# Seven block products for the spreads of layers 1 to 3, and layer 0's candidate kept in PSUM

## The chip, the cores and the metric

The kernel runs on one core of a Trainium2 chip. The metric is device time in microseconds (us), from the start of a launch to its end; a profiled span is about 1.8 us shorter than the time of the same run.

## The reference, cut to what matters

64 samples of 256 nodes by 128 features pass through four graph layers in float32. Each layer ends in a residual layer norm. All samples share one 256x256 adjacency matrix.

```python
# layer 0, five steps (in_matrix = out_matrix = adj)
m  = einsum('nm,bmd->bnd', adj, h)               # "spread"
z  = sigmoid(av @ w3.T + u3(h)); r = sigmoid(av @ w4.T + u3(h))
hv = tanh(av @ w5.T + (r * h) @ u5.T)            # "candidate"
h  = (1 - z) * h + z * hv
# layer 1: one spread over the off-diagonal weights    (q1 in the kernel)
# layer 2: attention, then one spread over A_final     (g)
# layer 3: adj, adj^2 and adj^3 applied to x, weighted (q3 is the first)
x = layernorm(x + layer(x))                      # after every layer
```

## The kernel before: what the change and the argument touch

The samples are taken in 32 pairs. The kernel first lists all its operations, each with one or more ways (engine, expected microseconds, function). A planner inside the kernel then puts them into one fixed order, with one fixed tile for each value. Two of its tables:

```python
CLASSES = {"X": (512, 15), ..., "A": (512, 30), ..., "PS": (512, 8), ...}   # tiles: size, how many
USES = {"DVE+": ("DVE", "PORT"), "POOL": ("POOL", "PORT"), "POOL-": ("POOL",)}
```

`X` holds the 15 pairs in flight, `A` the shared SBUF tiles, `PS` eight tiles of PSUM, the banks (SBUF and PSUM are the memories in which the kernel has its tiles; all 7196 pass records of the kernel before write PSUM). A way marked `DVE+` is a VectorE operation on two SBUF operands, but for some normalizations and relus on one. The planner books it on VectorE and on a PORT, which GpSimd's sums use too: it never plans the two for the same time.

A spread comes in two forms. The plain one is two batches by two block rows, each against 256 columns. The other, in the manner of Strassen and Winograd, takes seven block products of 128 columns, with sums of blocks before, between and after them:

```python
def spread(i, right):                    # 4 products of 256 columns
    t = bank()
    for b in range(2):
        def fn(b=b):
            for j in range(2):
                nc.tensor.matmul(t.at(2, N)[:, b, :], tokens(i)[:, 2*b+j, :], right.ap[:, j, :], ...)
        pe(mm(512), fn, [i, right, *[t] * b], [t])
    return t

def spread7(h, right, terms):            # 7 products of 128 columns
    sv, o, t = Value("A", name="sums"), Value("A", name="mT"), bank()
    def sum_(us, us_pool, fn, r, w):
        S.add([("DVE+", us, ...), ("POOL", us_pool, ...)], r, w)
    sum_(...)  sum_(...)  sum_(...)                        # sums of h
    product(0) product(1) product(3) product(2)            # into the four quarters of one bank
    evacuate(o <- t)                                       # copy, ScalarE or VectorE
    sum_(sv <- o, o)
    product(0) product(3) product(1)                       # on top of the same bank
    sum_(o3 <- sv, sv);  evacuate(o0 <- t0);  dve(o1, o2 <- t1, t3, sv)
    return o
```

A spread of this form is called a seven below. Before the change only layer 0 used `spread7`, in 150 places; the other 106 spreads were plain. The end of a step of layer 0 was:

```python
act(tanh: hv <- t)                       # bank t is free from here on
dve2(hv <- hv - hT)                      # dve2 = "DVE+": SBUF, SBUF
dve2(hv <- (z + 1) * hv)
dve2(hT <- 0.5 * hv + hT)
```

## Time and profile before

| | before |
|---|---|
| time | 1494.5 us (1494.3 to 1494.62, 3 runs) |
| TensorE busy | 1485.7 of 1493.0 us, 7196 pass records |
| VectorE, ScalarE, GpSimd busy | 1227.4, 974.7, 701.5 us |
| passes of 128, 256, 512 columns, start to start | 0.1117, 0.216, 0.43 us |

A float32 product leaves two pass records: the 106 plain spreads, 424 products, left 848. The end of a matmul record is modelled and reaches past the start of the next (records of 128, 256 and 512 columns last 275, 379 and 592 ns, each 0.163 us more than their spacing), so a busy share near 100% can hide short pauses. The sound way is to take the distance from start to start for each width and to add these up. What is left over are pauses.

### The profile page before, as it was taken

The numbers are of one execution on the slowest core, as the hardware profiler recorded it, in microseconds if no ns is written. First come the engines' busy times: TensorE is split into PE (matmuls) and PEld (weight loads), VectorE is DVE, ScalarE is ACT, GpSimd is POOL, SyncE is SP. The second block draws the span as 40 slices with busy tenths as digits, with TensorE's granted clock in tenths as the row PEclk, the third lists the DMA queues.
The fourth block names the chain that finished last, engine by engine and source line by source line (L and its number), as shares of the span: only waits on it lengthen the run. The fifth ranks groups of instructions, "written<-read, shape, count | busy, mean of one in ns | idle before, by whom it ended". The sixth has DMA issues, their size and how long they took to land.

```text
span 1493.0 us, 26228 instructions
## 1 busy us (share of the span) xinstructions
PE 1485.7 (100%) x7196; PEld 1058.8 (71%) x7196; DVE 1227.4 (82%) x3041; ACT 974.7 (65%) x2860; POOL 701.5 (47%) x964
## 2 busy tenths in 40 slices
PE   9999999999999999999999999999999999999998
PEld 6555666666677777767667677776677767788997
DVE  7776988999989888887888888788788887889752
ACT  3444555666677776766666767577576667777874
POOL 3432543565566544445354444444345534356442
PEclk9999999999999999999999999999999999999999
DMA  8553556778789887777668876867678766677862
GB/s 233 109 107 74 118 120 128 142 145 160 157 162 177 163 179 152 151 162 160 135 135 170 154 143 132 169 150 164 138 142 163 157 136 135 130 147 164 160 125 64
DMA packets 949475, 217.02 MB, mean 145 GB/s; under 512 B 728144, under 2 KB 944848, under 8 KB 949328
## 3 DMA queue, kind: packets, MB, share of 16 engines
q1 hardware_dynamic: 949328, 215.34, 71.2%
q8 instruction: 58, 0.95, 0.3%
q14 instruction: 89, 0.73, 0.2%
HBM read 117.12 MB, written 98.11 MB: 144 GB/s over the span
## 4 chain that ended last, share of the span: by engine, by line
PE 100%; POOLq 0%; ACT 0%; DVE 0%; issue 0%; ACTq 0%; POOL 0%
PE ps L563 16%; PE ps L545 12%; PE ps L689 9%; PE ps L696 9%; PE ps L681 9%; PE ps L697 9%; PE ps L682 9%; PE ps L718 8%; PE ps L788 4%; PE ps L832 4%; PE ps L824 4%; PE ps L825 4%; PE ps L748 2%; PE ps L520 0%; PE ps L295 0%; PE ps L456 0%
## 5 line engine op out<-in xcount | busy, mean ns | idle before, releaser
L235 ACT COPY a<-ps 128x512 f32<-128x512 f32 (+2 forms) x465 | 210.8, 461 | 166.7 <-PE ps L545 48.3
L563 PEld LDWEIGHTS ps<-aTt,a 128*128 128x128 f32 x1140 | 167.8, 192 | 45.2 <-issue 38.0
L685 ACT ACTIVATE a<-ps,bzrh 128x512 f32<-128x512 f32 x160 | 109.8, 686 | 121.9 <-PE ps L682 105.2
L563 PE MATMUL ps<-aTt,a 128*128 128x128 f32 x1140 | 188.9, 275 | 0.0
L699 ACT ACTIVATE a<-ps,bzrh 128x512 f32<-128x512 f32 x160 | 109.9, 687 | 112.2 <-PE ps L697 107.2
L696 PE MATMUL ps<-a,w 128*128 128x512 f32 x320 | 163.6, 593 | 0.0
L697 PE MATMUL ps<-a,u5h 128*128 128x512 f32 x320 | 163.4, 592 | 0.0
L682 PE MATMUL ps<-a,w 128*128 128x512 f32 x320 | 163.4, 592 | 0.0
L689 PE MATMUL ps<-a,w 128*128 128x512 f32 x320 | 162.4, 593 | 0.0
L582 POOL TENSOR_TENSOR a<-a 128x128 f32<-128x128 f32 x132 | 80.9, 614 | 168.1 <-DVE a L578 154.4
L642 ACT ACTIVATE a<-ps 128x128 f32<-128x128 f32 x460 | 121.1, 282 | 54.9 <-PE ps L788 26.0
L563 PEld LDWEIGHTS ps<-aT,a 128*128 128x128 f32 x780 | 125.1, 191 | 42.2 <-issue 36.6
L526 DVE STREAM_TRANSPOSE a<-a 128x512 f32<-128x512 f32 x217 | 150.7, 698 | 4.8 <-PE ps L689 1.0
L718 PEld LDWEIGHTS ps<-W,a 128*128 128x128 f32 x1024 | 135.9, 192 | 20.7 <-issue 17.9
L718 PE MATMUL ps<-W,a 128*128 128x128 f32 x1024 | 147.1, 275 | 0.0
L563 PE MATMUL ps<-aT,a 128*128 128x128 f32 x780 | 144.9, 275 | 0.0
L650 POOL TENSOR_TENSOR s<-s,neg_half 128x4 f32<-128x4 f32 x128 | 138.6, 1083 | 8.7
L691 ACT ACTIVATE a<-ps,bzrh 128x512 f32<-128x512 f32 x160 | 110.4, 691 | 41.3 <-PE ps L689 34.5
L681 PE MATMUL ps<-a,W 128*128 128x512 f32 x256 | 130.8, 593 | 0.0
L702 DVE SCALAR_TENSOR_TENSOR a<-a,a 128x512 f32<-128x512 f32 x160 | 115.1, 721 | 7.8 <-ACT a L691 6.1
L584 DVE TENSOR_TENSOR a<-ps,a 128x256 f32<-128x256 f32 x150 | 62.6, 418 | 70.3 <-ACT a L235 45.4
L570 POOL TENSOR_TENSOR a<-a,a 128x128 f32<-128x128 f32 x100 | 59.3, 593 | 119.9 <-DVE a L569 89.9
(198 smaller groups left out, 3303.4 us busy)
## 6 DMA issues: line engine op xcount, KB each, us to landing
e<-a SPq DMA_DIRECT2D x278, 256.0 KB, 2.7
a<-e SPq DMA_DIRECT2D x1112, 64.0 KB, 2.3
e<-b SPq DMA_DIRECT2D x32, 512.0 KB, 3.3
b<-e SPq DMA_DIRECT2D x128, 128.0 KB, 3.6
x<-x_in SPq DMA_DIRECT2D x32, 256.0 KB, 4.3
t<-xT_in SPq DMA_DIRECT2D x32, 256.0 KB, 5.3
a<-d SPq DMA_DIRECT2D x32, 256.0 KB, 3.6
y_out<-a SPq DMA_DIRECT2D x32, 256.0 KB, 2.4
```

The source lines that it names most:

```text
L235: S.add([("ACT", us[0], lambda: nc.scalar.copy(o(), i())), ("DVE", us[1], lambda: nc.vector.tensor_copy(o(), i()))], r, w)
L526: dve(n / 512 * 0.55 + 0.09, lambda: nc.vector.transpose(st.at(n), i.at(n)), [i], [st])
L545: nc.tensor.matmul(t.at(2, N)[:, b, :], tokens(i)[:, 2 * b + j, :], right.ap[:, j, :], start=(b == j == 0), stop=(j == 1), skip_group_chec ...
L563: pe(mm(128), lambda: nc.tensor.matmul(blk(t, k), left(), rt(), start=start, stop=True, skip_group_check=True), [*r, right, terms, *[t] * ...
L642: nc.scalar.activation(tokens(junk)[:, c, :], v.at(len(tiles), D)[:, k, :], AF.Square, scale=D ** -0.5, accum_out=mv()[:, c, 1:2])
L650: pool(1.02, lambda: nc.gpsimd.tensor_tensor(rs(), rs(), neg_half.ap, op=ALU.pow), [s, neg_half], [s])
L681: nc.tensor.matmul(t.at(512), mat("u3"), hT.at(512), start=True, stop=False)
L682: nc.tensor.matmul(t.at(512), w4.ap, mT.at(512), start=False, stop=True)
L689: pe(mm(512), lambda t=t, mT=mT: nc.tensor.matmul(t.at(512), w3.ap, mT.at(512), start=False, stop=True, skip_group_check=True), [w3, mT, t ...
L696: nc.tensor.matmul(t.at(512), w5.ap, mT.at(512), start=True, stop=False)
L697: nc.tensor.matmul(t.at(512), u5h.ap, r.at(512), start=False, stop=True)
L718: nc.tensor.matmul(tokens(t)[:, c, :], tokens(i)[:, c, :], w(), start=(first and k == c == 0), stop=(k == len(lefts) - 1), skip_group_chec ...
```

## The change

The intent is fewer columns through TensorE: q1, g and q3 take the seven-product form in the first 28 pairs, 84 spreads in all. To make room beside TensorE, the candidate of layer 0 stays in its PSUM bank through the tanh, the difference and the product, as operations with at most one SBUF operand. Some constants of the planner move with it: `BY_DMA` says for how many of the last pairs TensorE, and not a transfer, transposes a value (four transposes, a turn), and `SPARE` is a charge in us on a way.

```diff
-BY_DMA = {"h": 1, "y": 0, "x1": 0, "x2": 3, ...}
+BY_DMA = {"h": 1, "y": 2, "x1": 0, "x2": 2, ...}
+SEVEN = {"q1": 4, "g": 4, "q3": 4}          # the last 4 pairs keep the plain form
-"B": (1024, 5)
+"B": (1024, 6)
-SPARE = {"DVE": 0.6, "DVE+": 0.0, "POOL": -0.3}
+SPARE = {"DVE": 1.0, "DVE+": 0.0, "POOL": -0.3}
...
+    aT7, offT7, ginT7 = winograd(aT, "aT7"), winograd(offT, "offT7"), winograd(ginT, "ginT7")
...
-            act(0.59, ... activation(hv.at(512), t.at(512), AF.Tanh, ...), [t, bzrh], [hv])
-            dve2(TT, ... tensor_sub(hv, hv, hT), [hv, hT], [hv])
-            dve2(TT, ... scalar_tensor_tensor(hv, z, 1.0, hv, add, mult), [hv, z], [hv])
-            dve2(TT, ... scalar_tensor_tensor(new, hv, 0.5, hT, mult, add), [hv, hT], [new])
+            act(0.59, ... activation(t.at(512), t.at(512), AF.Tanh, ...), [t, bzrh], [t])
+            dve(TT, ... tensor_sub(t, t, hT), [t, hT], [t])
+            dve(TT, ... scalar_tensor_tensor(t, z, 1.0, t, add, mult), [t, z], [t])
+            dve(TT, ... scalar_tensor_tensor(new, t, 0.5, hT, mult, add), [t, hT], [new])
...
-        qT = to_sbuf(spread(x1, offT), "qT")
+        qT = spread7(x1, offT, offT7) if S.pair < n_pairs - SEVEN["q1"] else to_sbuf(spread(x1, offT), "qT")
         (the same for g in layer 2 with ginT7, and for q3 in layer 3 with aT7)
```

More of the change, by code (lines that the diff above doesn't have):

```diff
@@ L16 @@
 STEPS = 5
-BY_DMA = {"h": 1, "y": 0, "x1": 0, "x2": 3, "w": 0, "z": 3, "x3": 0}
+BY_DMA = {"h": 1, "y": 2, "x1": 0, "x2": 2, "w": 0, "z": 3, "x3": 0}
 WARM = 4
 FAST = (0, 1, 2, 3, 4)
+SEVEN = {"q1": 4, "g": 4, "q3": 4}
 FIRST, FINAL = 2, 0
@@ L37 @@
 ROWS = ["l1_bias", "bp", "b1", "gat_g", "gat_b", "b2"]
-CLASSES = {"X": (512, 15), "T": (512, 4), "A": (512, 30), "H": (520, 6), "B": (1024, 5), "S": (32, 64), "PS": (512, 8), "D": (512, 4), "E": (1024, 8)}
+CLASSES = {"X": (512, 15), "T": (512, 4), "A": (512, 30), "H": (520, 6), "B": (1024, 6), "S": (32, 64), "PS": (512, 8), "D": (512, 4), "E": (1024, 8)}
 SEEN = {"PE": 0.23, "ACT": 0.16, "DVE": 0.16, "POOL": 0.12, "SP": 0.0}
@@ L463, with winograd @@
     dve(0.25, lambda: nc.vector.tensor_add(vq.ap[:, 1, :], mat("v3"), mat("v6")), [W1], [vq])
-    aTt = fixed([4, P], "aTt")
-    blk_a = lambda j, i: aT.ap[:, j, i * P:(i + 1) * P]
-    dve(0.25, lambda: nc.vector.tensor_sub(aTt.ap[:, 0, :], blk_a(0, 1), blk_a(0, 0)), [aT], [aTt])
-    for k, other in ((1, lambda: aTt.ap[:, 0, :]), (2, lambda: blk_a(0, 1))):
-        dve(0.25, lambda k=k, other=other: nc.vector.scalar_tensor_tensor(aTt.ap[:, k, :], blk_a(1, 1), -1.0, other(),
-                                                                         op0=ALU.mult, op1=ALU.subtract), [aT, aTt], [aTt])
-    dve(0.25, lambda: nc.vector.tensor_add(aTt.ap[:, 3, :], aTt.ap[:, 1, :], blk_a(1, 0)), [aT, aTt], [aTt])
+    def winograd(v, name):
+        o, blk = fixed([4, P], name), lambda j, i: v.ap[:, j, i * P:(i + 1) * P]
+        dve(0.25, lambda: nc.vector.tensor_sub(o.ap[:, 0, :], blk(0, 1), blk(0, 0)), [v], [o])
+        for k, other in ((1, lambda: o.ap[:, 0, :]), (2, lambda: blk(0, 1))):
+            dve(0.25, lambda k=k, other=other: nc.vector.scalar_tensor_tensor(o.ap[:, k, :], blk(1, 1), -1.0, other(),
+                                                                             op0=ALU.mult, op1=ALU.subtract), [v, o], [o])
+        dve(0.25, lambda: nc.vector.tensor_add(o.ap[:, 3, :], o.ap[:, 1, :], blk(1, 0)), [v, o], [o])
+        return o
+    aT7, offT7, ginT7 = winograd(aT, "aT7"), winograd(offT, "offT7"), winograd(ginT, "ginT7")
     centre(vx, lambda: vx.ap, 2)
@@ L676, in layer0 @@
         for s in range(STEPS):
-            mT = spread7(h, aT, aTt) if s in FAST and FIRST <= S.pair < n_pairs - FINAL else to_sbuf(spread(h, aT), "mT")
+            mT = spread7(h, aT, aT7) if s in FAST and FIRST <= S.pair < n_pairs - FINAL else to_sbuf(spread(h, aT), "mT")
             t = bank()
@@ L683, in layer0 @@
             pe(mm(1024), reset, [Wg, w4, hT, mT], [t])
-            r, z, hv, new = (Value("A", name=n) for n in ("r", "z", "hv", "hT"))
+            r, z, new = (Value("A", name=n) for n in ("r", "z", "hT"))
             act(0.59, lambda t=t, r=r: nc.scalar.activation(r.at(512), t.at(512), AF.Tanh, bias=bzrh.ap[:, 1:2], scale=0.5),
@@ L698, in layer0 @@
             pe(mm(1024), candidate, [w5, u5h, mT, r], [t])
-            act(0.59, lambda t=t, hv=hv: nc.scalar.activation(hv.at(512), t.at(512), AF.Tanh, bias=bzrh.ap[:, 2:3]),
-                [t, bzrh], [hv])
-            dve2(TT, lambda hv=hv, hT=hT: nc.vector.tensor_sub(hv.at(512), hv.at(512), hT.at(512)), [hv, hT], [hv])
-            dve2(TT, lambda hv=hv, z=z: nc.vector.scalar_tensor_tensor(hv.at(512), z.at(512), 1.0, hv.at(512),
-                                                                      op0=ALU.add, op1=ALU.mult), [hv, z], [hv])
-            dve2(TT, lambda hv=hv, hT=hT, new=new: nc.vector.scalar_tensor_tensor(
-                new.at(512), hv.at(512), 0.5, hT.at(512), op0=ALU.mult, op1=ALU.add), [hv, hT], [new])
+            act(0.59, lambda t=t: nc.scalar.activation(t.at(512), t.at(512), AF.Tanh, bias=bzrh.ap[:, 2:3]), [t, bzrh], [t])
+            dve(TT, lambda t=t, hT=hT: nc.vector.tensor_sub(t.at(512), t.at(512), hT.at(512)), [t, hT], [t])
+            dve(TT, lambda t=t, z=z: nc.vector.scalar_tensor_tensor(t.at(512), z.at(512), 1.0, t.at(512),
+                                                                   op0=ALU.add, op1=ALU.mult), [t, z], [t])
+            dve(TT, lambda t=t, hT=hT, new=new: nc.vector.scalar_tensor_tensor(
+                new.at(512), t.at(512), 0.5, hT.at(512), op0=ALU.mult, op1=ALU.add), [t, hT], [new])
             hT = new
@@ L798, in layer2 @@
         dve_or_pool(lambda e: e.tensor_add(tokens(hb), tokens(hg), row("b2", 4)), [hg, rbc], [hb])
-        gT = to_sbuf(spread(hg, ginT), "gT")
+        gT = spread7(hg, ginT, ginT7) if S.pair < n_pairs - SEVEN["g"] else to_sbuf(spread(hg, ginT), "gT")
         t, z = seed((0.49, 0.61), tokens, lambda: row("b1", 4), [rbc, gT]), Value("A", name="z")
@@ L812, in layer3 @@
         xT = turn(x3, "xT", "x3")
-        qT = to_sbuf(spread(x3, aT), "qT")
+        qT = spread7(x3, aT, aT7) if S.pair < n_pairs - SEVEN["q3"] else to_sbuf(spread(x3, aT), "qT")
         rr, o = Value("A", name="rr"), Value("A", name="o")
```

## The prediction

> **What bounds the kernel now.** I read the page first: busy shares, the slices and the chain that ended last.
>
> ```profile
> span 1493.0 us, 26228 instructions
> PE 1485.7 (100%) x7196; PEld 1058.8 (71%) x7196; DVE 1227.4 (82%) x3041; ACT 974.7 (65%) x2860; POOL 701.5 (47%) x964
> ...
> PE   9999999999999999999999999999999999999998
> ...
> PEclk9999999999999999999999999999999999999999
> ...
> PE 100%; POOLq 0%; ACT 0%; DVE 0%; issue 0%; ACTq 0%; POOL 0%
> ```
>
> The chain is TensorE from one end to the other, at full clock. But a modelled matmul end (a record outlasts the start of the next) can hide a short pause, so busy time alone doesn't prove that the array never waits. I went on to the timeline of TensorE and to the chain in order of time, where a piece lasts from its start to the start of the next. They show the spacing of each shape:
>
> ```profile
> 758.34 1.03 PE L545 MATMUL ps<-ginT,a 128*128 128x256 f32 x4
> 759.21 1.03 PE L545 MATMUL ps<-aT,x 128*128 128x256 f32 x4
> 760.07 1.03 PE L545 MATMUL ps<-ginT,a 128*128 128x256 f32 x4
> 760.93 1.03 PE L545 MATMUL ps<-aT,x 128*128 128x256 f32 x4
> 761.80 1.05 PE L788 MATMUL ps<-h,b 128*128 128x128 f32 x8
> ```
>
> ```profile
> 26.19 2.01 PE ps L563 x18
> 758.51 3.46 PE ps L545 x16
> 761.96 0.89 PE ps L788 x8
> ```
>
> A float32 product leaves two records (two passes). A pass of 256 columns costs 3.46/16 = 0.216 us; a pass of 128 columns costs 2.01/18 = 0.1117 us, and 0.89/8 = 0.111 in another line of the program. From the timeline around 705 us, a pass of 512 columns starts 0.43 us after the one before (1.72 us for four). The price list explains the span. Block products of 128 or 130 columns: (1140+780+120+60 of the sevens, 1024, 512, 256) = 3892 records x 0.1117 = 435 us. Passes of 256: (272+256+256+64 of the spreads, three times 256 in layer 3) = 1616 x 0.216 = 349 us. Passes of 512: 320 for each of five products in the gates = 1600 x 0.429 = 686 us. With 40 transposes and the setup (about 10 us with the warm-up) that is some 1480 us of 1493, and the rest is the first microseconds and the drain at the end. So TensorE streams without pauses, and only fewer or shorter passes, or a shorter start or end, can shorten the kernel. The waits of TensorE itself and the windows agree:
>
> ```profile
> PE ps L295 <- DVE ones L293: 1.2, 1, 1.2
> ```
>
> ```profile
> 0.00:40.00 40.00, 38.80 (x167) 26.51 (x168) 29.78 (x75) 15.79 (x27) 16.47 (x30) 1.00 0.83 223
> 300.00:700.00 400.00, 400.00 (x2009) 285.17 (x2008) 354.60 (x870) 278.36 (x846) 214.62 (x282) 1.00 0.81 161
> 700.00:1100.00 400.00, 400.00 (x1942) 283.31 (x1941) 331.12 (x831) 265.75 (x766) 182.64 (x257) 1.00 0.73 149
> 1450.00:1493.00 43.00, 36.88 (x184) 32.13 (x182) 10.42 (x39) 21.84 (x83) 11.17 (x18) 0.99 0.34 80
> ```
>
> The columns are the stretch, its length, then PE, PEld, DVE, ACT and POOL busy. Only the first and last stretch have idle TensorE, 1.2 and 6.1 us. The second engine is VectorE: 354.60 of 400 us, 89%, from 300 to 700 us. That is the engine to fear.
>
> [...] Each of our passes has its own load (7196 of both), and a 128-column pass is spaced 0.1117 us: [...] a narrow pass pays more than half of a wide one, 0.1117 against 0.216/2 = 0.108 us; which part of it binds, no row here tells. This is why seven products do not cost 7/8 of eight.
>
> [...] VectorE's 128x512 two-tensor operations on SBUF average 721 to 774 ns, the ones with a PSUM operand (line 807) 680 ns; GpSimd's 128x128 sums average 584 to 614 ns, though single ones in the timeline took 450.
>
> [...] 128x256 TENSOR_TENSOR takes 418 ns from PSUM and 427 ns from SBUF. I use the trace.
>
> [...] no row of before shows a wait of TensorE for a bank.
>
> **The change part by part.**
>
> 1. The spreads of layers 1, 2 and 3 (q1, g, q3) go from two batches of two block rows by a 256-column operand, eight passes of 256 columns, to seven block products, fourteen passes of 128. Before: 8 x 0.216 = 1.73 us. After: 14 x 0.1117 = 1.56 us. Saved: 0.166 us each. Three spreads in 28 of the 32 pairs (the last four keep the old form) are 84: 84 x 0.166 = 13.9 us. All of it lies on the path, as TensorE is the path. The naive count, one block product in eight gone, would be 84 x 2 x 0.1117 = 18.8 us; I don't believe it, because each remaining product is narrower.
>
> 2. PE transposes: y takes TensorE for two pairs more, x2 for one pair less. Net one turn of four transposes, estimated at 0.11 us each from the passes of the same width: +0.4 us.
>
> 3. Added elementwise work of a seven: seen from the 150 sevens of before, each has a 128x256 difference (93 of 150 on VectorE at 0.43, else GpSimd at 0.85), two 128x128 sums (39 of 300 on VectorE at 0.28, else GpSimd at 0.6), a 128x256 sum (99 of 150 on VectorE at 0.43, else GpSimd at 0.88), a 128x128 sum (18 of 150 on VectorE at 0.34, else GpSimd at 0.61), one VectorE operation at 0.418, and an additional ScalarE copy of 0.266. Per seven: VectorE 0.27+0.07+0.28+0.04+0.42 = 1.08 us, GpSimd 0.32+1.03+0.30+0.54 = 2.2 us. Times 84: VectorE +91, GpSimd +184, ScalarE +22 us, all beside TensorE if they keep up.
>
> 4. Layer 0's three operations after the candidate (lines 701, 702, 704; 480 instructions) read PSUM: at 0.68 to 0.70 in place of 0.72 to 0.76 us that is about 480 x 0.04 = -19 us on VectorE[...]. The tanh (0.687 us x160) stays in length; writing PSUM instead of SBUF shows no penalty (128x512 copies: 597 ns to PSUM, 587 from it).
>
> 5. The larger spare charge on VectorE shifts what has a choice to ScalarE: at most the 79 scalings of PSUM (0.41 us) and 52 statistics (0.28 and 0.16), some 55 us. I put down -25.
>
> VectorE then: 1227+91-19-25 = 1274 us, 86% of 1481. ScalarE about 1025, 69%. GpSimd about 885, 60%. None is above TensorE.
>
> 6. Setup: two more sets of four VectorE sums of 128x128, under 3 us of VectorE work, needed first for layer 1, whose products come after 180 us. Nothing on the path.
>
> Sum: 1494.5 - 13.9 + 0.4 = 1481.0 us. For a changed static order, with more work per pair beside TensorE, I add 0.5: **1481.5 us**, 0.9% less.
>
> **The rivals.**
>
> VectorE becomes a second bound. From 300 to 700 us it has 354.6 of 400. The stretch has 216 records of line 545, so 27 spreads: 27 x 1.08 = 29 us more, some 6 less from layer 0: 378 of 395 us, 96%, if nothing moves to other engines. A static order with 96% on an engine would make TensorE wait here and there. For it: this sum. Against it: many pairs are in flight (15 tiles of x), ScalarE has 30% left in the stretch and GpSimd 46%, the freed port and the higher charge move work there, and 700 to 1100 us is at 83%. It would give back 3 to 15 us: 1484 to 1496.
>
> PSUM banks run out. The candidate's bank was free after the tanh; now three more VectorE operations hold it, at least 2.1 us, with queueing I estimate 4. 160 x 4 = 640 us over 1481 is 0.4 of a bank of eight, and a seven holds its bank over a copy, a sum and a second round of products. For it: all eight banks are one pool. Against it: TensorE has no wait for a bank now. If it bites: 3 to 10 us of pauses, 1484 to 1491.
>
> The full eighth is gained: if the spacing of the sevens were not tied to the width, 18.8 us saved, 1476. The rows of line 563 speak against it.
>
> The end moves: the last 43 us hold 6 us of idle TensorE, and the new use of transposes for y and x2 is aimed at the last pairs. Worth plus or minus 2 us.
>
> **Range and chances.** The term of 13.9 us rests on spacings which are constant to a per cent, so the low end is that sum with 2 us gained at the end: 1478.5. Upwards there are the two waits, each of which I give one chance in five or so, mostly small: 1487. To be faster by 2% the kernel would have to reach 1464.6, 30 us less, where even the naive count gives 19: 0.01. Slower by 2% is 1524, when VectorE would have to grow by a fifth: 0.01. Within 2%: 0.98.
>
> **What would show it.** The count of matmul records: line 563's should rise by 84 x 14 = 1176 and line 545's fall by 84 x 8 = 672; with four transposes, 7196 becomes 7704. Passes of 128 columns still about 0.111 us apart, the chain still nearly all PE, and no idle TensorE in windows between 40 and 1400 us. VectorE near 1274 us, with the three operations of layer 0 near 0.69 us and the tanh near 0.69; GpSimd near 885, its 128x128 sums shorter than 0.6. I am wrong if TensorE shows waits for VectorE or for banks amid the run, if the passes of the sevens are spaced wider than 0.112 us, if PSUM-to-PSUM operations are much slower than 0.7 us, or if the start or the tail lengthens by more than 3 us.

## The result

The changed kernel took 1486.85 us (1485.46 to 1488.05, 4 runs) against 1494.4 us in the same rounds (1494.23 to 1494.62, 4 runs). The ratio is 0.9949, with a 95% interval from 0.9932 to 0.9966. All ratios here are the mean time of one kernel's fast runs over that of the other's of the same rounds, so not quite the ratio of the medians. The gain is 7.5 us of the 13.0 predicted; the time lies in the range, 0.15 us below its upper end.

The head of the changed kernel's page and the shares of its chain:

```profile
span 1485.2 us, 28119 instructions
...
PE 1474.5 (99%) x7704; PEld 1062.6 (72%) x7704; DVE 1234.4 (83%) x3083; ACT 1026.9 (69%) x3116; POOL 829.8 (56%) x1307
...
PE 95%; DVE 2%; DMA 1%; ACT 0%; issue 0%; SPq 0%; POOL 0%; POOLq 0%; ACTq 0%; DVEq 0%
```

The 7704 records are those predicted. But the chain, PE to the last per cent before, is PE to 95% now: at times something else decides. Adding up the passes of both traces at the spacing of their width (0.1116, 0.2159 and 0.4292 us for 128, 256 and 512 columns, 0.1118 for 130, 0.1092 for a transpose) shows where the gain went:

| us | before | after | difference | predicted |
|---|---|---|---|---|
| passes at their spacing | 1481.85 | 1468.45 | -13.4 | -13.5 |
| pauses between passes, the slow first passes among them | 3.5 | 9.2 | +5.7 | +0.5 |
| ahead of the first pass and behind the last (rest of the span) | 7.6 | 7.6 | 0 | 0 |
| span | 1493.0 | 1485.2 | -7.8 | -13.0 |

The first passes are slow: of 256 columns one starts every 0.427 us until 6.9 us in before and until 4.4 us in after, and then every 0.216 us. With a wait of 0.2 us for a load of x in after, that is 3.0 us of the pauses in before and 2.3 in after, all in the first 10 us. The new pauses have places: 3.4 us between 400 and 500 us, 2.0 us between 1300 and 1400 us, 0.9 us after 1450 us (0.3 of it there before too). The windows show the first two (stretch, length, busy time of PE, PEld, DVE, ACT, POOL, clock, DMA share, GB/s), first of before, then of after:

```profile
400.00:500.00 100.00, 100.00 (x511) 70.85 (x510) 90.87 (x236) 74.92 (x218) 60.70 (x79) 1.00 0.87 167
```

```profile
400.00:500.00 100.00, 97.94 (x538) 69.02 (x537) 93.11 (x232) 76.49 (x236) 71.33 (x110) 1.00 0.87 167
500.00:600.00 100.00, 100.00 (x551) 74.29 (x552) 91.11 (x231) 77.72 (x243) 72.02 (x111) 1.00 0.81 167
1300.00:1400.00 100.00, 99.01 (x654) 87.16 (x653) 90.61 (x279) 81.41 (x307) 67.69 (x97) 1.00 0.73 148
```

The second column after the stretch, PE, was at 100 and now isn't. Compare the columns of VectorE: 90.87 against 93.11, and 91.11 in the next stretch, where nothing waits. A window alone doesn't name VectorE as the cause. The waits of TensorE in the changed kernel (total, times, longest) had one line before and have eight now:

```profile
PE ps L296 <- DVE ones L294: 1.2, 1, 1.2
PE ps L751 <- DVE a L810: 0.9, 1, 0.9
PE ps L566 <- ACT a L236: 0.7, 1, 0.7
PE ps L566 <- DMA a<-e: 0.5, 1, 0.5
PE ps L566 <- DMA x<-x_in: 0.5, 1, 0.5
PE ps L566 <- DVE a L572: 0.4, 1, 0.4
PE ps L828 <- ACT a L236: 0.3, 1, 0.3
PE ps L548 <- DMA x<-x_in: 0.2, 1, 0.2
```

The first is the old wait at the start. The others are single short ones, most of them ahead of a seven (L566, its products), on ScalarE copies, VectorE, and transfers. The chain in order of time (start, length, what) shows how one such pause arises:

```profile
465.21 0.67 DVE a L707
...
466.09 3.94 DMA x<-x_in
...
470.16 2.28 PE ps L566 x18
...
472.47 0.59 ACT a L236
...
473.10 0.94 PE ps L566 x6
```

At 466.09 a load of x starts. It is that of pair 15, the first pair that must reuse one of the 15 tiles of x; before it the order waits for a VectorE operation. The load takes 3.94 us, and the seven starts at its end. TensorE had other passes until 469.5 us, so the pause is only 0.7 us. The chain ahead of the load, from 425 to 466 us, is VectorE's for 29.8 of 41 us and transfers' for 7.9. At 472.47 a copy of ScalarE, in the midst of a seven, holds TensorE again.

### The profile page after: what moved, and what is told of

It reads as the page before. It is cut to its first block, busy times and chain, and to the rows that moved or that the text cites.

```text
span 1485.2 us, 28119 instructions
## 1 busy us (share of the span) xinstructions
PE 1474.5 (99%) x7704; PEld 1062.6 (72%) x7704; DVE 1234.4 (83%) x3083; ACT 1026.9 (69%) x3116; POOL 829.8 (56%) x1307
## 4 chain that ended last, share of the span: by engine, by line
PE 95%; DVE 2%; DMA 1%; ACT 0%; issue 0%; SPq 0%; POOL 0%; POOLq 0%; ACTq 0%; DVEq 0%
PE ps L566 23%; PE ps L699 9%; PE ps L700 9%; PE ps L684 9%; PE ps L685 9%; PE ps L692 9%; PE ps L721 7%; PE ps L835 4%; PE ps L828 4%; PE ps L827 4%; PE ps L791 4%; PE ps L548 2%; PE ps L751 2%; DMA x<-x_in 1%; DMA a<-e 0%; DVE a L529 0%
## 5 line engine op out<-in xcount | busy, mean ns | idle before, releaser
L566 PEld LDWEIGHTS ps<-aT,a 128*128 128x128 f32 x2144 | 291.4, 192 | 83.3 <-issue 76.7
L236 ACT COPY a<-ps 128x128 f32<-128x128 f32 (+2 forms) x553 | 230.4, 433 | 137.8 <-PE ps L566 48.6
L566 PE MATMUL ps<-aT,a 128*128 128x128 f32 x2144 | 315.7, 275 | 0.9 <-DMA a<-e 0.5
L585 POOL TENSOR_TENSOR a<-a 128x128 f32<-128x128 f32 x205 | 103.7, 510 | 150.4 <-DVE a L581 110.6
L688 ACT ACTIVATE a<-ps,bzrh 128x512 f32<-128x512 f32 x160 | 110.0, 688 | 104.4 <-PE ps L685 90.7
L703 ACT ACTIVATE ps<-ps,bzrh 128x512 f32<-128x512 f32 x160 | 106.1, 663 | 105.3 <-PE ps L700 102.3
L700 PE MATMUL ps<-a,u5h 128*128 128x512 f32 x320 | 163.4, 592 | 0.0
L587 DVE TENSOR_TENSOR a<-ps,a 128x256 f32<-128x256 f32 x234 | 96.5, 416 | 67.8 <-ACT a L236 32.0
L721 PEld LDWEIGHTS ps<-W,a 128*128 128x128 f32 x1024 | 132.8, 192 | 16.1 <-issue 13.9
L694 ACT ACTIVATE a<-ps,bzrh 128x512 f32<-128x512 f32 x160 | 110.5, 691 | 45.2 <-PE ps L692 37.8
L685 PEld LDWEIGHTS ps<-a,w 128*128 128x128 f32 x320 | 60.8, 190 | 76.5 <-issue 68.1
L700 PEld LDWEIGHTS ps<-a,u5h 128*128 128x128 f32 x320 | 60.8, 190 | 76.5 <-issue 64.8
L705 DVE SCALAR_TENSOR_TENSOR ps<-a,ps 128x512 f32<-128x512 f32 x160 | 109.7, 686 | 6.1 <-ACT a L694 4.4
```

Of the source, the lines that this page charges most:

```text
L236: S.add([("ACT", us[0], lambda: nc.scalar.copy(o(), i())), ("DVE", us[1], lambda: nc.vector.tensor_copy(o(), i()))], r, w)
L566: pe(mm(128), lambda: nc.tensor.matmul(blk(t, k), left(), rt(), start=start, stop=True, skip_group_check=True), [*r, right, terms, *[t] * ...
L685: nc.tensor.matmul(t.at(512), w4.ap, mT.at(512), start=False, stop=True)
L694: act(0.59, lambda t=t, z=z: nc.scalar.activation(z.at(512), t.at(512), AF.Tanh, bias=bzrh.ap[:, 0:1], scale=0.5), [t, bzrh], [z])
L700: nc.tensor.matmul(t.at(512), u5h.ap, r.at(512), start=False, stop=True)
L721: nc.tensor.matmul(tokens(t)[:, c, :], tokens(i)[:, c, :], w(), start=(first and k == c == 0), stop=(k == len(lefts) - 1), skip_group_chec ...
```

## The experiments

After the result I had four theories, numbered in this order where the expectations give numbers. The first: VectorE is full in places. The second: PSUM banks are held too long. The third: inputs come late at the ends of longer chains, whatever engine or bank is full, the load of x at 466 us first of all. The fourth: the fixed order is a poor fit, planned with durations that the chip doesn't keep. Twelve kernels ran; times are medians, and all gave the right output except one. Its output is wrong, which doesn't matter for the time.

### Run 1: the changed kernel again

> The changed kernel once more, unedited, as a control for the edits of it and for a second trace. If the pauses of TensorE (5.8 us more than before, of which 3.4 us lie between 400 and 500 us) come from the static order and full engines, they are at the same places again: 1485 to 1488 us. If they came from chance (one late transfer in one run), the pauses of this trace lie elsewhere and the times spread by more than 2 us.

Measured: 1488.91 us (1486.99 to 1489.43, 5 runs) against 1494.77 us; 0.996 (0.9947 to 0.9972). The passes add up to 1468.45 us as before, the pauses to 11.7 us, again near 470, 473, 498 to 501, 1364 and 1390 us. Two small ones, 0.7 us together, are new, at 642 and 897 us. So the pauses belong mostly to the order, though their size varies, and the spread of over 2 us that I had expected of chance is there as well: the changed kernel spreads over some 2.5 us within a set of runs where the kernel before spread over 0.4 in the first set and 1.6 here. The second set, 2 us higher, also lies above my range.

### Runs 2 and 3: one half of the change each

Run 2 keeps the sevens and everything else, and puts the candidate back into SBUF:

```diff
-            act(0.59, ... activation(t.at(512), t.at(512), AF.Tanh, ...), [t, bzrh], [t])
-            dve(...) dve(...) dve(...)          # difference, product, new state, from PSUM
+            act(0.59, ... activation(hv.at(512), t.at(512), AF.Tanh, ...), [t, bzrh], [hv])
+            dve2(...) dve2(...) dve2(...)       # as before
```

> The changed kernel with layer 0's candidate back in an SBUF tile; its PSUM bank is free after the tanh again. TensorE's work is the same as in the changed kernel. Theory 1 (VectorE is full from 400 to 500 us, and the order slips behind its plan): VectorE gets some 20 us more work [...], so the pauses grow: 1488 to 1495 us. Theory 2 (the banks, held longer by the candidate, make TensorE wait): the pauses go, 1481 to 1483 us.

Run 3 keeps the candidate in PSUM and takes the 84 sevens out:

```diff
-SEVEN = {"q1": 4, "g": 4, "q3": 4}
+SEVEN = {"q1": 32, "g": 32, "q3": 32}
```

> The changed kernel with the old spreads in layers 1 to 3 for all pairs: the candidate in PSUM and the four constants remain. TensorE's work is that of the kernel before plus one turn, 0.4 us. Theory 1: with VectorE relieved and without the sums of the sevens there are no pauses, 1494 to 1496 us. Theory 2: the held banks make TensorE wait all the same, 1497 us or more.

Measured, all in the rounds of run 1:

| | candidate in SBUF | candidate in PSUM |
|---|---|---|
| plain spreads in layers 1 to 3 | 1494.77 (before) | 1495.12 (run 3) |
| sevens in layers 1 to 3 | 1514.0 (run 2) | 1488.91 (run 1) |

(Run 2: 1512.96 to 1516.79, ratio 1.0133, interval 1.012 to 1.0147. Run 3: 1494.86 to 1497.79, ratio 1.0009, interval 0.9995 to 1.0022. Before differs from run 3 in the planner's constants too.) This is the largest effect, and I had not foreseen it: the candidate in PSUM is worth nothing alone and 25.1 us together with the sevens; the sevens alone lose 19 us. Both theories that I had put against each other missed run 2 by far, on the same side.

The pass sum of run 2 is 1468.45 us, the same as after; its pauses are 36.4 us, of which 14.1 lie between 400 and 500 us and 10.8 between 1400 and 1450 us. Its page and two of its windows:

```profile
PE 1484.0 (98%) x7704; PEld 1066.0 (70%) x7704; DVE 1274.6 (84%) x3092; ACT 1032.5 (68%) x3149; POOL 882.8 (58%) x1255
```

```profile
400.00:500.00 100.00, 90.96 (x477) 62.38 (x477) 97.37 (x240) 70.24 (x218) 70.16 (x90) 1.00 0.81 163
1400.00:1440.00 40.00, 32.40 (x203) 28.97 (x203) 33.50 (x113) 35.20 (x135) 21.81 (x32) 0.97 0.76 150
```

VectorE and GpSimd stand at 1274.6 and 882.8 us, which are nearly the very figures that I had predicted for the whole change: by chance, as this run lacks the candidate's term. The page of run 3, and from the waits of TensorE the only one besides that at the start:

```profile
PE 1485.6 (99%) x7200; PEld 1058.5 (71%) x7200; DVE 1182.0 (79%) x2912; ACT 998.6 (67%) x2995; POOL 646.7 (43%) x991
```

```profile
PE ps L548 <- DVE s L610: 0.4, 1, 0.4
```

What makes the two halves depend on each other is seen in single durations. The candidate's difference, with minimum/median/maximum in ns, first in run 2, then in after:

```profile
L705 DVE TENSOR_TENSOR a<-a,a x128: 643/685/1589, 53.3 to 1373.4; 128x512 f32<-128x512 f32 x128
```

```profile
L704 DVE TENSOR_TENSOR ps<-ps,a x128: 659/690/700, 52.8 to 1352.6; 128x512 f32<-128x512 f32 x128
```

And from the groups of instructions (busy us, mean ns of one, then the idle time before them) one of GpSimd's sums in a seven, again run 2 and then after:

```profile
L585 POOL TENSOR_TENSOR a<-a 128x128 f32<-128x128 f32 x210 | 123.4, 591 | 184.5 <-DVE a L581 157.0 <-DVE s L786 5.6 <-DMA e<-a 4.8
```

```profile
L585 POOL TENSOR_TENSOR a<-a 128x128 f32<-128x128 f32 x205 | 103.7, 510 | 150.4 <-DVE a L581 110.6 <-DMA a<-e 22.8 <-DVE s L610 5.3
```

The medians are alike, 685 and 690 ns: PSUM isn't a faster place. The maximum is not: 1589 ns with two SBUF operands, 700 ns with one. Of all 480 operations of this kind in run 2 (difference, product, new state), 102 took over 750 ns, and each of these overlaps a two-tensor operation of GpSimd; of the 172 that overlap none, the longest took 695 ns. In after 347 of the 480 overlap one, and the longest took 700 ns. And GpSimd's sum takes 591 ns in the mean in run 2, 510 ns in after. So what lengthened is a VectorE operation on two SBUF operands beside a two-tensor operation of GpSimd, and in the mean GpSimd's sum with it; with one SBUF operand none of the 480 of after took over 700 ns. The planner keeps the same two kinds of work apart by its PORT. Matching every record to its operation, I added up the lengths of the records of the two kinds of work, `DVE+` and `POOL`, in each trace:

| us | VectorE, `DVE+` | GpSimd sums | both | share of the span |
|---|---|---|---|---|
| before | 848.5 | 434.9 | 1283.5 | 86% |
| run 3, candidate in PSUM | 490.9 | 397.0 | 887.9 | 59% |
| run 2, sevens | 913.8 | 614.3 | 1528.2 | 101% |
| after, both | 525.5 | 590.2 | 1115.7 | 75% |

The sevens ask for some 230 us of this shared time, moving the candidate frees some 400. These shares count a time twice where neighbouring records of one engine overlap, and stretched records at their stretched length. With each engine's time counted once they are about 81%, 57%, 95% and 71%, so without the move the two kinds of work would fill nearly the whole span if they never overlapped (on the chip some 280 us of them did overlap). The time of the chain from the end of the candidate's product to the new state, which each pair goes through five times, follows: 7.36 us before, 5.45 in run 3, 8.80 in run 2, 5.70 in after (means over 26 pairs). Run 3 gains nothing from a faster chain because TensorE, which sets its end, wasn't waiting. What no run separates is how much of run 2's loss comes from the contention on the chip and how much from the planner's own PORT rule, which spaces the work out ahead of time.

The planner can be run without the chip. It gives the plan's estimate and no measurement. Between 40 and 1440 us the plan itself leaves TensorE idle for 0.1 us in before, 3.0 in run 3, 13.2 in after and 43.5 in run 2. So run 2's loss stood in its plan before it ran. With the PORT rule taken out of run 2's plan alone, 15.0 us are left; whether the chip would keep to that plan is not shown. A rival is that the candidate in SBUF takes one shared tile more and that these run short. The plan doesn't support it: with 31, 32, 34 or 40 tiles in place of 30 run 2's plan leaves 47 to 57 us.

### Run 4: the plain spread, cut to the width of a seven

```diff
                 for j in range(2):
-                    matmul(t[:, b, :], tokens(i)[:, 2*b+j, :], right.ap[:, j, :], ...)
+                    for k in range(2):
+                        matmul(t[:, b, k*P:(k+1)*P], tokens(i)[:, 2*b+j, :], right.ap[:, j, k*P:(k+1)*P], ...)
```

This is the kernel before with sixteen passes of 128 columns where it had eight of 256.

> The kernel before, with each spread cut into sixteen passes of 128 columns in place of eight of 256: same products, same sums, only narrower. There are 106 such spreads (96 in layers 1 to 3, ten in layer 0). If a narrow pass costs 0.1117 us, as the trace of before has it, each spread takes 16 x 0.1117 - 8 x 0.216 = 0.06 us more: 1494.5 + 6.3 = 1500.8 us (1499 to 1502). If width costs nothing, so that the full eighth of 18.8 us is there to be had, 1494.5 us.

Measured: 1500.92 us (1500.61 to 1501.28), ratio 1.0043 (1.003 to 1.0055), a hit within 0.2 us. From its chain in order of time:

```profile
760.93 3.57 PE ps L546 x32
```

Two spreads of 16 passes, 0.1116 us each, 1.785 us a spread against 1.73 before. The narrowness costs 0.06 us a spread, and 106 of them cost 6.1 us. It confirms that seven narrow products save 0.17 us a spread and not the eighth, 0.22 us, that the count of products promises.

### Run 5: without the difference (wrong)

```diff
-            dve(TT, ... tensor_sub(t.at(512), t.at(512), hT.at(512)), [t, hT], [t])
```

> The changed kernel without the subtraction of the state from layer 0's candidate (a wrong result, on purpose): 160 VectorE operations of about 0.61 us from start to start are gone, nearly 100 us, and TensorE's products and ScalarE's work are the same. Theory 1 (VectorE is full in stretches and TensorE waits for what it makes): the pauses go, TensorE's spacing sum of 1468.4 us plus 3.5 us of pauses as before the change and the tail: 1480 to 1482 us. Theory 3 (the pauses come from tiles of x that are freed late, or from transfers): the waits for loads stay, 1484 us or more.

Measured: 1486.63 us (1485.29 to 1490.24), ratio 0.9951 (0.9938 to 0.9963). VectorE falls to 1169.4 us, 79%, and to 85.03 us in the window from 400 to 500 us, where after has 93.11:

```profile
400.00:500.00 100.00, 98.51 (x571) 72.26 (x570) 85.03 (x229) 76.85 (x237) 62.58 (x103) 1.00 0.84 167
```

TensorE still waits: 9.9 us of pauses in all, as in after. So VectorE's busy time isn't the one cause of the 5.7 us, and the first theory falls as the whole answer. As in all these runs the planner has made a new order for the edit, so single pauses can't be compared.

### Run 6: one more tile of x

```diff
-"X": (512, 15), ..., "A": (512, 30)
+"X": (512, 16), ..., "A": (512, 31)
```

> The changed kernel with 16 tiles for x in place of 15 and 31 shared tiles in place of 30 (without the latter the plan finds no order). Loads of x can be issued earlier. Theory 3 (late tiles of x): the pauses between 400 and 500 us shrink from 3.4 us to under 1, 1483 to 1485 us. Theory 1: the same VectorE work, so pauses of the same size, if not at the same places: 1485 to 1490 us.

Measured: 1490.83 us (1488.64 to 1491.52), ratio 0.9973 (0.9961 to 0.9986).

```profile
400.00:500.00 100.00, 100.00 (x544) 70.10 (x543) 93.12 (x229) 75.97 (x228) 71.99 (x107) 1.00 0.83 164
1300.00:1400.00 100.00, 97.27 (x623) 84.45 (x622) 89.67 (x284) 85.59 (x334) 68.00 (x96) 1.00 0.76 151
```

The pauses from 400 to 500 us go from 3.4 to 0.2 us, as the third theory said, with VectorE as full as in after (93.12). But 8.0 us of pauses lie between 1300 and 1450 us, where after had 2.0, and the whole is no faster (this interval overlaps that of run 1). This fits the cause named for that one pause, though the new order may have removed it too; its removal wasn't worth its length.

### Run 7: a wider margin in the plan

```diff
-MARGIN, LAG = 1.1, 0.3
+MARGIN, LAG = 1.15, 0.3
```

> The changed kernel with the planner's charge on every operation outside TensorE raised from 1.10 to 1.15 times its duration: the same instructions, in another static order, in which TensorE is given work whose inputs are ready later by plan. Theory 1 with slip (the order was planned with engines that are a little too quick): pauses shrink, 1481 to 1485 us. If VectorE simply lacks time in the stretch, no order helps: 1486 to 1492 us.

Measured: 1489.94 us (1489.22 to 1492.56), ratio 0.9975 (0.9963 to 0.9988): 12.2 us of pauses. If the order suffered only from durations planned too short, this should have helped. It didn't; but the plan with this margin itself leaves TensorE idle for 26.9 us (13.2 in after's), so the run doesn't settle the question.

### Run 8: more of the sums on GpSimd

```diff
-SPARE = {"DVE": 1.0, "DVE+": 0.0, "POOL": -0.3}
+SPARE = {"DVE": 1.0, "DVE+": 0.3, "POOL": -0.3}
```

> The changed kernel with 0.3 us charged in the plan on VectorE operations that GpSimd could take: more sums go to GpSimd. Theory 1: VectorE's busy time falls by 20 to 60 us and the pauses shrink, 1482 to 1486 us; if GpSimd's slower and contended sums come too late instead, 1488 us or more.

Measured: 1492.64 us (1491.57 to 1494.68), ratio 0.9991 (0.9977 to 1.0005). VectorE has 1157.5 us, even less than in run 5, GpSimd 985.4, and TensorE pauses for 14.9 us, 9.1 of them between 400 and 500 us. Less work on VectorE and more on GpSimd made it worse. That GpSimd's slower sums (a 128x256 difference takes 766 ns there and 434 on VectorE in after; a 128x128 sum of GpSimd 632 ns in the mean where its record overlaps a VectorE operation on SBUF operands alone, 460 ns elsewhere) hold up the products is argued only; the waits of TensorE name a copy of ScalarE first and a sum of GpSimd with little:

```profile
PE ps L721 <- ACT ps L236: 3.1, 3, 1.6
...
PE ps L566 <- POOL a L572: 0.3, 1, 0.3
```

### Runs 9 and 10: other orders

Many settings of the planner's constants were tried in its own estimate. The plan of after leaves TensorE idle for 13.2 us in that estimate, run 9's for 4.7. Run 10 has 82 sevens instead of 84.

```diff
 (run 9)  "A" 30 -> 31; SPARE 0.9, 0, -0.4; DUE 15.5, LAST 11; MARGIN, LAG = 1.08, 0.28; HOLD (1.05, -18.8, 0, 40)
 (run 10) BY_DMA y 0, x2 3; SEVEN 5, 5, 4; "A" 31, "B" 5; SPARE 0.6, -0.1, -0.3; DUE 15.5, LAST_DUE 11
```

> The changed kernel with six constants of its planner moved and one shared tile more: the same products, sums and copies, in another static order, chosen from some 2900 plans because the planner itself leaves TensorE idle for 4.7 us between 40 and 1440 us, against 13.2 us in its plan for the changed kernel. Theory 4 (the pauses are set by the static order: it places products at times when their bank or input isn't free by plan, and the chip follows the plan): the pauses shrink to 2 to 5 us, 1482 to 1485 us. If the pauses come from slips that no plan foresees (the charges of this plan are lower, so its slack is smaller), 1486 to 1491 us.

> The changed kernel in another order again, with the same charges as the changed kernel (1.10 and 0.3 us): 5.9 us of idle TensorE in its plan between 40 and 1440 us; two sevens fewer, y never and x2 in three pairs turned on TensorE. TensorE's spacing sum is within 0.5 us of the changed kernel's. Theory 4: 1482 to 1486 us. Slips: 1487 us or more.

Measured: run 9 1487.24 us (1483.89 to 1487.89, 5 runs), ratio 0.9946 (0.9933 to 0.996), with 8.7 us of pauses; run 10 1492.09 us (1490.53 to 1493.85, 21 runs), ratio 0.9985 (0.9978 to 0.9991), with 14.5 us. A better plan by its own measure gave the same time or a worse one. Run 9 ties with the changed kernel; no run beats it clearly.

### Run 11: one bank less

```diff
-"PS": (512, 8)
+"PS": (512, 7)
```

> The changed kernel planned for seven PSUM banks in place of eight, all else equal. Theory 2 in its weaker form (all eight banks are in use in the crowded stretches, and a product waits until a reader has freed one): pauses grow by 8 to 18 us, 1495 to 1505 us. If the banks have room and only VectorE's lack of time matters, 1486 to 1490 us.

Measured: 1494.35 us (1493.01 to 1496.87, 13 runs), ratio 1.0 (0.9992 to 1.0008): 5.4 us above the changed kernel in run 1 and 7.5 above its first set, between the two expectations and nearer to that of the banks. The whole gain is gone. Its two longest waits, though, are put down to other things than banks:

```profile
PE ps L566 <- ACT x L665: 1.5, 1, 1.5
PE ps L827 <- DMA a<-e: 1.4, 1, 1.4
```

Taking each pause of over 0.05 us and asking what ended last ahead of it, the former use of its bank or an input, some 6.4 us of run 11 fall to banks, 2.8 to transfers, 1.0 to ScalarE. For after the same count says: banks 1.6, transfers 1.5, ScalarE 0.8, VectorE 0.5 us. (A transfer is inferred there, where all else had long been done.) So banks are dear now, but not the only thing.

### Run 12: the banks freed first

```diff
                 late = self.due(op.pair) - op.rest + HOLD[op.layer] if op.pair >= 0 else -1e4
+                late -= 15.0 * any(v.cls == "PS" and v.ap is not None for v in op.holds)
                 key = (way[1], late, op.number)
```

Of the operations that can start at the same time, the plan now prefers those that work on a bank already held.

> The changed kernel with one line more in its planner: among operations that can start equally early, those that work on a PSUM bank already in use go 15 us ahead in urgency, so that open banks are finished and freed before new ones are opened. Same instructions' work, all constants and charges kept. Pairing the trace's records with the program's order gave 6.25 banks in use on average between 40 and 1440 us in the changed kernel (6.6 from 400 to 500 us, all eight there for 23% of the time) against 5.53 in the kernel before. Theory 2 in its weaker form (the banks are full because their readers come late): the occupancy falls below 5.5 and the pauses to between 4 and 6.5 us of which 3.5 are there before the change too: 1481.5 to 1484.5 us. If pauses come from late inputs whatever the banks do: occupancy falls and the time stays at 1486 us or more.

Measured: 1488.64 us (1487.24 to 1490.5), ratio 0.996 (0.9947 to 0.9974). The edit did what it should: the mean number of banks in use between 40 and 1440 us falls from 6.25 to 4.57 (5.53 before the change), and all eight are in use for 1.6% of the time in place of 12%. No pause is a bank's any more. Yet the pauses add up to 11.1 us, and these are the longest waits:

```profile
PE ps L567 <- ACT a L666: 1.5, 1, 1.5
PE ps L567 <- DMA x<-x_in: 1.3, 1, 1.3
...
PE ps L567 <- DMA a<-e: 0.8, 1, 0.8
```

By the same count 4.9 us are transfers and 1.05 us ScalarE. So freeing the banks doesn't bring back the 5.7 us; that they run out is not its one cause.

## Why the prediction was right or wrong, by its own steps

**The bound and the price of the passes: right, to 0.1 us.** TensorE sets the end in both kernels (100% and 95% of their chains). The passes were to give -13.9 for the sevens and +0.4 for a turn; the two traces give -13.4 together. The turn alone is the +0.44 us in the pass sum of run 3 (1482.29 against 1481.85). The rival that the full eighth is gained is out, by run 4. Why a narrow pass costs more than half of a wide one (0.1116 us against half of 0.2159, 3.4% more per column) stays open: the load records of the trace of after last 190 to 192 ns in the mean ahead of narrow and wide passes alike (192 at L566, 190 at L700), so they don't tell the two apart.

**The added elementwise work: right for two engines, too large for VectorE.** Run 3 splits the sum. From run 3 to after, the 84 sevens added 183 us to GpSimd (predicted 184) and 28 us to ScalarE (22), but 52 us to VectorE, where I had 91. From before to run 3, VectorE lost 45 us, and the two terms for the candidate and for the spare charge made 44. GpSimd lost 55 us there, for which I had no term. So both totals came out below mine, VectorE at 1234 us for 1274 and GpSimd at 830 for 885.

**The candidate in PSUM: right in sign, far too small in meaning.** I booked it as 19 us of VectorE's time, off the path, and gave no price to what it spares GpSimd's sums (those of L585 take 591 ns in run 2 and 510 in after). By the four kernels of runs 1 to 3 it carries the change: without it the sevens lose 19 us, with it they gain 6. A sum of busy time per engine doesn't show this. The sum over the planner's PORT hints at it: 95% of the span against 71%. (Two readings of the prediction here were selective: 128x512 operations on two SBUF operands averaged 678 to 805 ns by group in the trace of before, not 721 to 774, and one group of GpSimd's 128x128 sums 644 ns.)

**"None is above TensorE", and so only 0.5 us for the changed order: this step failed.** The order gave back 5.7 us in the first trace, 8.2 in the second (11.7 against 3.5), in short pauses in a few places. That takes nearly all of the difference between 1481.5 and 1486.85. The prediction's own sign of being wrong came true: TensorE waits for VectorE amid the run (0.9 us at L751, 0.4 us at L566), and windows between 40 and 1400 us have idle TensorE (97.94 of 100 us). That the time still lay in the range, by 0.15 us, was luck: the second set lies 1.9 us above it. An engine needn't be above TensorE for such pauses: VectorE was busy for 1234.4 us of 1485.2.

**The rivals.** I gave VectorE as a second bound one chance in five, with 378 of 395 us between 300 and 700 us. It stood at 356 of 400 there, hardly more than before, and run 5 rules its busy time out as the one cause. For the banks I had estimated 4 us more on the candidate's, 0.4 of a bank: the mean hold of a candidate's bank went from 2.86 us to 7.27, times 160 over 1485 us 0.47 of a bank. Run 11 shows that the reserve is gone, run 12 that banks alone aren't it. The end neither gained nor lost: 7.6 us outside the passes in both.

**What stays open.** Each single remedy (VectorE in run 5, the tile of x in run 6, the margin in run 7, the order in runs 9 and 10, the banks in run 12) moved or exchanged pauses and left a sum of 8.7 to 14.5 us. That fits one picture: a seven is two rounds of products with a copy and sums between them, so 84 more of them stretch chains everywhere, and in a fixed order the first late link holds TensorE, whichever it is. The picture is argued; no run isolates it. The plans support a part of it. Beside the pauses of the traces, the idle time of TensorE in the plan between 40 and 1440 us (the estimate of the section on runs 2 and 3) is:

| us | before | run 3 | run 9 | run 12 | run 10 | run 5 | after | run 8 | run 6 | run 7 | run 11 | run 2 |
|---|---|---|---|---|---|---|---|---|---|---|---|---|
| idle in the plan | 0.1 | 3.0 | 4.7 | 5.1 | 5.9 | 7.7 | 13.2 | 19.5 | 19.6 | 26.9 | 27.2 | 43.5 |
| pauses on the chip | 3.5 | 3.4 | 8.7 | 11.1 | 14.5 | 9.9 | 9.2 | 14.9 | 13.8 | 12.2 | 15.2 | 36.4 |

The two go together only roughly. In after's plan TensorE is idle from 465 to 472 us and from 1358 to 1391 us, where two of the three groups of pauses between 40 and 1400 us lie; near 499 us it isn't. So a part of the 5.7 us was planned and could have been read off the plan before the run, and a part came on the chip. That the run-to-run spread grew because TensorE now waits at times for transfers is argued as well.

## What to carry to other kernels

Price an exchange of work between engines not only per engine but per shared resource: add up what needs the same port, bank or tile, with and without the change, before asking whether any engine is full. Two halves of a change can be worthless or harmful alone and pay together, so run all four combinations. Where a program plans its own order, look also at what the plan leaves idle. And where an engine streams without pauses, a saving of its work arrives in full only if no new pauses come with it (here 13.4 us of passes gave 7.8 us of the span); take the distance from start to start, as the busy share hides 0.163 us of each pause here (the longest of after, 1.015 us, shows as 0.852).
